# The sums with v inside a chunk: from vector products and reductions to small TensorE products, woven among the large ones

## The chip, the cores and the metric

The kernel runs on one core of one Trainium2 chip. The metric is the device time of one execution in microseconds (us). Runs are timed several times and the median is given; beside them stands one execution taken with the hardware profiler, whose rows are used below. The engines are TensorE (PE in the profile; PEld is its weight load), VectorE (DVE), ScalarE (ACT), GpSimd (POOL) and the queue SP, which issues all transfers of this kernel.

## What is computed

Eight sequences (batches) of 256 tokens with 512 features pass through a transformer layer (self attention, cross attention with a context, a feed-forward block of 2048) and then through a layer of the RWKV kind. All of it is float32. The change lies in the recurrence of the second layer, which has 32 heads of 16 channels:

```python
def step(s, rkvw):                      # s: one 16 x 16 state per batch and head
    r_t, k_t, v_t, w_t = rkvw           # u, a fixed factor per channel
    a = k_t[..., :, None] * v_t[..., None, :]
    out = jnp.einsum('bhi,bhij->bhj', r_t, u * a + s)
    s = a + w_t[..., :, None] * s
    return (s, out)
_, out = jax.lax.scan(step, s0, rkvw)   # over the 256 tokens
```

Then `out` is normalized per head, multiplied by a gate `g`, projected by `Wo` and added to the input (the time mix); a second normalization, a shift by one token and three 512 x 512 products follow (the channel mix). r, k, v, g come from 512 x 512 products, the decay w from a small two-step product.

## The kernel before

The whole program is unrolled. Every instruction carries a priority; a list scheduler orders each engine's instructions when the program is built: where several are ready by its clock, the lowest priority number goes first. On the chip each engine then follows its list in order, and SP its list of transfers.

First come the 32 jobs of the transformer layer (four phases of eight batches), then the second layer, in stages per batch that are named by a letter. `SEQ` (L71) gives the order in which the stages are written down; `AT` and `PACE` (L85, L86) set their priorities: stage s of batch b stands at `PACE * (b + AT[s])` from a common base. In the time mix (`TimeMix`, L539 to L847):

- **a**: normalization, transposition, the low-rank mixing coefficients (L564, L566, L575).
- **b**: gate g and product k. **e**: product v, decay w (L667, L675), product r. Each 512 x 512 product of 256 tokens is written as three products of rounded parts (`mm3`, L185 to L187): 72 with 512 columns and 48 with 256 columns in one batch. k, v, r and w go to DRAM.
- **c**: the 256 tokens are cut into 16 chunks of 16; a partition holds one chunk of four heads (8 x 16 = 128 partitions). For every chunk, GpSimd multiplies r, k and the decays and VectorE sums over the channels, which gives `A`, the 16 x 16 lower triangle of coefficients between the tokens of the chunk, for four heads (L713 to L749; four levels m = 1, 2, 4, 8). Then, for each token t of a chunk, GpSimd multiplies row t of `A` with the t + 1 values of v so far (L755), and VectorE sums (L762): this is the part of `out` that stems from the own chunk. It goes to DRAM as `on`, with the scaled k (`ks`), the scaled r (`r0`) and the decay of a chunk (`dd`).
- **d**, the stage between chunks: the states of all chunks from small 32 x 32 products of k and v (L807), a scan over the chunks on VectorE (L824), 32 x 32 products of r with the states (L834), added to `on` under a mask for the two chunks that share 32 partitions (L837), then the norm per head (L839 to L847) and the store of `yg`.

The channel mix has stages **f** (gate, product o, normalization, mixing) and **g** (products fr, fk, fv and the result); f waits for `yg` of its batch.

SBUF is dealt out by hand: `SLOTS` names the buffers that a tile of a phase may take, `BANKS` the PSUM banks. A tile that is given a taken buffer waits until the last reader of the old tile is done. Stage d has one PSUM bank `wtp` and two banks `up`; `A` has one buffer; the tiles `in` (k, r, w and v of stage c) have four.

An fp32 matmul (L807, L834, L564, L566, L667, L675, L780) stands in the profile as two matmul records, a product of rounded parts as one.

## Time and profile before

| | us |
|---|---|
| median of 3 runs (lowest, highest) | 1974.78 (1973.81, 1986.49) |
| profiled execution, its own time | 1982.31 |
| its span, first to last instruction | 1980.5 |
| second layer: stage b of batch 0 begins (first L652) | 1193.7 |
| last product of stage e, batch 7, copied out (last L643) | 1641.2 |
| stage c: first L713, last L762 | 1239.2, 1794.4 |
| last L834 of stage d, batch 7 | 1819.1 |

From 1193 us to the end the engines are busy: PE 655, DVE 581, POOL 527, ACT 366 of 787.5 us. Busy time of PE is a union of records that overlap, so it is no measure of how much the array does; at half the clock the same product is busy for almost twice as long. The granted clock (1.0 or 0.5 in stretches of 3.41 us, or multiples) is read from the clock column of a table by stages, and from the distance of the starts of two equal products in the timeline. Idle time of an engine costs nothing where another one is the bottleneck.

| first start per batch, us | 0 | 1 | 2 | 3 | 4 | 5 | 6 | 7 |
|---|---|---|---|---|---|---|---|---|
| b (L652) | 1194 | 1242 | 1289 | 1343 | 1405 | 1470 | 1528 | 1593 |
| c (L713) | 1239 | 1311 | 1383 | 1454 | 1521 | 1589 | 1662 | 1728 |
| d (L807) | 1323 | 1395 | 1462 | 1529 | 1599 | 1670 | 1736 | 1779 |
| g (L924) | 1690 | 1742 | 1791 | 1830 | 1863 | 1896 | 1929 | 1962 |

### The profile page before, as it was taken

To read this page: it belongs to the slowest core of one execution; us is meant where nothing else is said; L and a number is where in the kernel's file an instruction comes from. 1 tells how busy PE (TensorE), PEld (TensorE's weight loads), DVE (VectorE), ACT (ScalarE), POOL (GpSimd) and SP (SyncE) were. 2 spreads that over 40 slices of the span, in tenths; PEclk is the share of its full clock that TensorE was granted. 3 is DMA by queue.
4 is the path that set the end of the run, shared out by engine and by line. 5 is a ranking of instruction groups with operands and counts; after the bars stand their busy time and mean duration, and the time that the engine had idled before them with its cause. 6 is when DMAs were issued, how large, how long until landed. Compare 5 with 4: busy or idle time off the path is not lost.

```text
span 1980.5 us, 38765 instructions
## 1 busy us (share of the span) xinstructions
PE 1756.4 (89%) x14576; PEld 1471.8 (74%) x14576; DVE 1379.7 (70%) x3211; ACT 1106.5 (56%) x2745; POOL 747.5 (38%) x550
## 2 busy tenths in 40 slices
PE   4999999989999998999999988888889895789877
PEld 4777777777777776799999976676777673677766
DVE  4777777776778687665654454669678788888554
ACT  3877777887778688532332334354464454355342
POOL 2111111121221221232311100898899999992000
PEclk9999999999999999999999998988898886888888
DMA  6644444656555556322311133454556476442210
GB/s 189 158 125 119 118 118 125 190 142 164 132 146 143 133 135 207 110 90 69 107 65 64 54 128 103 116 142 125 157 138 165 130 195 184 142 108 97 75 64 22
DMA packets 237170, 247.35 MB, mean 125 GB/s; under 512 B 156292, under 2 KB 159244, under 8 KB 236983
## 3 DMA queue, kind: packets, MB, share of 16 engines
q1 hardware_dynamic: 236982, 244.87, 44.7%
q8 instruction: 115, 1.88, 0.4%
q14 instruction: 73, 0.59, 0.1%
HBM read 118.71 MB, written 58.98 MB: 90 GB/s over the span
## 4 chain that ended last, share of the span: by engine, by line
PE 60%; DVE 15%; DMA 6%; ACT 6%; POOL 5%; issue 3%; SPq 3%; POOLq 0%; DVEq 0%; ACTq 0%
PE o L185 8%; PE o L186 8%; PE o L187 8%; PE mm L185 5%; PE mm L186 4%; PE mm L187 4%; PE tr L366 3%; PE out L187 3%; PE out L186 3%; PE out L185 3%; DVE e L359 3%; POOL X L755 2%; PE cx L375 2%; DVE e L357 2%; PE sc L355 2%
## 5 line engine op out<-in xcount | busy, mean ns | idle before, releaser
L362 ACT ACTIVATE e<-e,mx 128x256 f32<-128x256 f32 x512 | 256.7, 506 | 43.0 <-DVE mx L359 42.0
L357 DVE TENSOR_TENSOR e<-sc,mc 128x512 f32<-128x512 f32 x256 | 172.1, 683 | 111.8 <-PE sc L355 56.2
L227 POOL TENSOR_TENSOR u<-y,u 128x1024 fp32r<-128x1024 f32 x32 | 78.5, 2452 | 440.8 <-ACT u L226 440.6
L359 DVE CUSTOM_DVE_ANT_0 e<-e,mn 128x256 f32<-128x256 f32 x512 | 220.6, 473 | 1.0
L755 POOL TENSOR_TENSOR X<-A,in 128x128 f32<-128x128 f32 (+14 forms) x120 | 209.3, 1779 | 14.7 <-DVE ob L762 12.4
L185 PE MATMUL o<-whi,s 128*128 128x512 f32 x320 | 148.4, 464 | 49.4 <-ACT s L890 31.8
L366 PE MATMUL tr<-ident,e 128*128 128x128 f32 x1024 | 174.7, 285 | 18.0 <-ACT e L362 14.7
L185 PE MATMUL mm<-u,whi 128*128 128x256 f32 x512 | 153.7, 301 | 14.3 <-DVE s L319 7.8
L370 ACT COPY pt<-tr 128x512 f32<-128x512 f32 x256 | 147.0, 582 | 34.6 <-PE tr L366 33.9
L366 PEld LDWEIGHTS tr<-ident,e 128*128 128x128 f32 x1024 | 122.3, 144 | 49.2 <-ACT e L362 24.2
L186 PE MATMUL mm<-u,whi 128*128 128x256 f32 x512 | 147.5, 288 | 4.0 <-POOL u L227 4.0
L185 PE MATMUL o<-u,whi 128*128 128x256 f32 x512 | 144.7, 287 | 3.1 <-ACT whi L171 1.6
L187 PE MATMUL mm<-u,wlo 128*128 128x256 f32 x512 | 147.0, 287 | 0.0
L186 PE MATMUL o<-u,whi 128*128 128x256 f32 x512 | 144.0, 283 | 0.0
L187 PE MATMUL o<-u,wlo 128*128 128x256 f32 x512 | 144.0, 283 | 0.0
L186 PE MATMUL o<-wlo,s 128*128 128x512 f32 x320 | 141.4, 442 | 0.0
L293 POOL TENSOR_TENSOR xr<-xr,row 128x512 f32<-128x512 f32 x48 | 65.7, 1388 | 186.0 <-DMA xr<-in_x 81.1
L355 PE MATMUL sc<-stk 128*128 128x256 f32 x512 | 118.0, 322 | 19.3 <-DVE e L357 13.9
L187 PE MATMUL o<-whi,s 128*128 128x512 f32 x320 | 134.4, 438 | 0.6 <-DVE s L891 0.5
L507 ACT ACTIVATE hf<-o,cv 128x256 f32<-128x256 f32 x128 | 59.8, 475 | 117.8 <-PE o L187 115.0
L197 POOL TENSOR_SCALAR rstd<-mv 128x2 f32<-128x2 f32 x48 | 17.2, 357 | 281.2 <-DVE mv L195 260.5
L185 PEld LDWEIGHTS o<-whi,s 128*128 128x128 f32 x320 | 70.0, 219 | 68.8 <-ACT s L890 33.3
(324 smaller groups left out, 5296.3 us busy)
## 6 DMA issues: line engine op xcount, KB each, us to landing
stk<-s SPq DMA_DIRECT2D x512, 128.0 KB, 2.4
x<-x SPq DMA_DIRECT2D x40, 512.0 KB, 4.7
x<-xr SPq DMA_DIRECT2D x24, 512.0 KB, 3.6
xr<-x SPq DMA_DIRECT2D x16, 512.0 KB, 4.8
w<-in_w SPq DMA_DIRECT2D x16, 512.0 KB, 6.7
w<-v SPq DMA_DIRECT2D x32, 256.0 KB, 3.2
x<-in_x SPq DMA_DIRECT2D x8, 512.0 KB
xr<-in_x SPq DMA_DIRECT2D x8, 512.0 KB, 3.6
```

The source lines that it names most:

```text
L185: TE.matmul(o, ah, bh, start=first, stop=False)
L186: TE.matmul(o, ah, bl, start=False, stop=False)
L187: TE.matmul(o, al, bh, start=False, stop=last)
L227: (eng or V).tensor_tensor(lo, y, r32(hi), ALU.subtract)
L293: G.tensor_tensor(x[:, t, :], x[:, t, :], r, ALU.add)
L355: TE.matmul(sc[:, t, :], qs[hm][:, hc, t * P : (t + 1) * P], ks[hm][:, hc, :], start=True, stop=True)
L357: V.tensor_tensor(e, sc, mc, ALU.mult)
L359: V.tensor_tensor_reduce(e[:, t, :], e[:, t, :], mn[:, t, :], 1.0, 3.0e38, ALU.add, ALU.min, accum_out=mx[:, kk2, hc, t : t + 1])
L362: S.activation(pr[:, t, :], e[:, t, :], AF.Exp, bias=mx[:, kk2, hc, t : t + 1], scale=-1.0, accum_out=sums[:, kk2, hc, t : t + 1])
L366: TE.transpose(pt_ps[:, kk, t * P : (t + 1) * P], pr[:, t, kk * P : (kk + 1) * P], ident)
L370: S.copy(pt, pt_ps)
L755: G.tensor_tensor(Y.rearrange("p (h j s) -> p h j s", h=4, j=16), A[:, t, 0:n, :].rearrange("p s h -> p h s").unsqueeze(2).broadcast_to([P ...
```

## The change

In stage c the products and sums with v (L755, L762), the transposed copy of v (L703) with its transfers, and the store of `on` are gone. `A` is now one tile for all batches, zeroed once, so that its upper triangle stays zero; it is laid out by column and goes to DRAM. The tile `in` has three buffers instead of four. In stage d the part of `out` from the own chunk is a product: for each half t of the tokens (128 rows), each of 32 heads and each group pr of 32 partitions (two chunks), a 32 x 32 block of `Ax` (the two triangles of a pair of chunks, spread by ScalarE with a mask so that the other quadrants are zero) by 32 x 16 values of v, into one bank: 2 x 32 x 4 = 256 fp32 matmuls per batch. A group pr takes rows and output partitions 32 pr to 32 pr + 31.

Stage d becomes a generator. `weave` only puts it on a list; `between(n)`, called in the k loops of the large products of all phases, counts their columns and emits the next piece of the generator when as many columns have gone by as the last `yield` asked for. The pieces take the priority of the stage that they are woven into. The yields of one batch add up to about 54,000 columns, the products of stages b and e of a batch have about 53,000. Stage f of batch b first emits what is left of d up to b (`finish`). `SEQ`, `AT` and `PACE` are set anew: with 4000 numbers between batches, the priorities follow the order in which the stages are written.

```diff
-        "in:a16-a19 ob:a12 vm:a20,a21 r0t:a22 sts:a23 on_:a2 "
+        "in:a16-a18 At:a19 Ax:a12 vm:a20,a21 r0t:a22 sts:a23 on_:a2 "
...
-    "a0 b0 a1 e0 c0 b1 a2 e1 c1 d0 b2 a3 e2 c2 d1 b3 a4 e3 c3 d2 b4 a5 e4 c4 d3 b5 a6 e5 c5 d4 b6 a7 e6 c6 d5 b7 "
-    "e7 c7 f0 d6 f1 g0 d7 f2 g1 f3 g2 f4 g3 f5 g4 f6 g5 f7 g6 g7"
+    "a0 b0 a1 e0 c0 b1 a2 e1 c1 b2 a3 d0 e2 c2 b3 a4 d1 e3 c3 b4 a5 d2 e4 c4 b5 a6 d3 e5 c5 b6 a7 d4 e6 c6 b7 d5 e7 c7 "
+    "f0 d6 f1 g0 f2 d7 g1 f3 g2 f4 g3 f5 g4 f6 g5 f7 g6 g7"
...
-AT = {"a": -0.5, "b": -8.75, "e": 1.8, "c": -9.5, "d": -9.3, "f": 6.25, "g": 7.75}
-PACE = 1000
+AT = {"a": -0.75, "b": 0, "e": 0.5, "c": 1, "d": 0, "f": 8.6, "g": 9.7}
+PACE = 4000
...
+    woven, columns = [], [0]
+    def between(n):
+        columns[0] += n
+        while woven and columns[0] >= woven[0][1]:
+            columns[0] -= woven[0][1]
+            was, phase[0] = phase[0], "time"
+            woven[0][1] = next(woven[0][2], None)
+            if woven[0][1] is None:
+                woven.pop(0)
+            phase[0] = was
+    def weave(b, steps):
+        if not woven:
+            columns[0] = 0
+        woven.append([b, 0, steps])
+    def finish(b):
+        while woven and woven[0][0] <= b:
+            columns[0] = woven[0][1]
+            between(0)
...
                     mm3(o[:, oo, :], wh[:, k, cs], wl[:, k, cs], xh[:, k, :], xl[:, k, :], k == 0, k == KC - 1)
+                    between(3 * T)
...
                     mm3(o, xh[:, k, ts], xl[:, k, ts], wh[:, k, :], wl[:, k, :], u == 0 and k == 0, u == n - 1 and k == KC - 1)
+                    between(3 * D)
...
                 TE.matmul(tp_[0:64, 0, :], d1[:, k, :], y[:, k, :], start=k == 0, stop=k == KC - 1)
+                between(4 * T)
...
-            vt = wt("in", [P, 64, 16])
-            for h in range(2):
-                vh = staged([P, 8, 64])
-                nc.sync.dma_start(out=vh, in_=vd.rearrange("e (c t) d -> (e c) t d", t=16)[:, 8 * h : 8 * h + 8, :])
-                S.copy(vt[:, :, 8 * h : 8 * h + 8].rearrange("p d s -> p s d"), vh)
-
-
-            A = wt("A", [P, 16, 16, 4])
+            if b == 0:
+                self.A = wt("A", [P, 16, 4, 16])
+                G.memset(self.A, 0.0)
+            A = self.A
...
-                return bass.AP(A.tensor, A.offset + 64 * t + 4 * s_, [A.ap[0], *dims])
+                return bass.AP(A.tensor, A.offset + 64 * s_ + t, [A.ap[0], *dims])
...
-            V.tensor_reduce(part(0, 0, [[68, 16], [1, 4]]), X.rearrange("p (t g i) -> p t g i", t=16, i=16), AX.X, ALU.add)
+            V.tensor_reduce(part(0, 0, [[65, 16], [16, 4]]), X.rearrange("p (t g i) -> p t g i", t=16, i=16), AX.X, ALU.add)
...
-            ob = wt("ob", [P, 16, 64])
-            for t in range(16):
-                n = t + 1
-                Y = wt("X", [P, 1024])[:, : 64 * n] if t else ob[:, 0, :]
-                G.tensor_tensor(
-                    Y.rearrange("p (h j s) -> p h j s", h=4, j=16),
-                    A[:, t, 0:n, :].rearrange("p s h -> p h s").unsqueeze(2).broadcast_to([P, 4, 16, n]),
-                    vt[:, :, 0:n].rearrange("p (h j) s -> p h j s", j=16),
-                    ALU.mult,
-                )
-                if t:
-                    V.tensor_reduce(ob[:, t, :], Y.rearrange("p (d s) -> p d s", s=n), AX.X, ALU.add)
+            ad = dtile(f"ad_{b}", [P, 16, 64])
+            nc.sync.dma_start(out=ad, in_=A.rearrange("p s h t -> p s (h t)"))
...
-            return back(kb, "ks"), back(rb, "r0"), dd, vd, back(ob, "on")
+            return back(kb, "ks"), back(rb, "r0"), dd, vd, ad
 
         def d(self, b, got):
-
-            ksd, r0d, dd, vd, ond = got
+            weave(b, self.steps(b, got))
+        def steps(self, b, got):
+            ksd, r0d, dd, vd, ad = got
             dn = staged([16, D])
             nc.sync.dma_start(out=dn.rearrange("c (e d) -> c e d", e=8), in_=dd.rearrange("e c d -> c e d"))
+            s0t = wt("s0t", [P, KC, 16])
+            nc.sync.dma_start(out=s0t, in_=a["ctx"][b, 2:18, :].rearrange("r (a j) -> (r a) j", j=16).rearrange("(g p) j -> p g j", p=P))
+            ks = [self.n_tile(ksd, t, "ks") for t in range(2)]
+            At = wt("At", [P, 2, 8, 64])
+            for t in range(2):
+                nc.sync.dma_start(out=At[:, t], in_=ad.rearrange("(e u c) s x -> u (c s) e x", e=8, u=2)[t])
+            r0 = [self.n_tile(r0d, t) for t in range(2)]
+            o = wt("on_", [P, 2, D])
+            yield 8 * T
...
+            r0t = wt("r0t", [P, KC, T])
+            yield 4 * T
+            for k2 in range(2):
+                tp = bank("wtp", [P, 2, T])
+                for kk in range(2):
+                    for t in range(2):
+                        TE.transpose(tp[:, kk, t * P : (t + 1) * P], r0[t][:, (2 * k2 + kk) * P : (2 * k2 + kk + 1) * P], ident)
+                S.copy(r0t[:, 2 * k2 : 2 * k2 + 2, :], tp)
+                if not k2:
+                    yield 8 * T
+            vms, vns = [], []
+            for t in range(2):
+                vms.append(wt("vm", [P, 2, D]))
+                vns.append(self.n_tile(vd, t))
+                for par in range(2):
+                    S.activation(vms[t][:, par, :], vns[t], AF.Copy, scale=pm[:, 2 + par : 3 + par])
+            def spread(t):
+                Ax = wt("Ax", [P, 32, 2, 16])
+                for par in range(2):
+                    S.activation(Ax[:, :, par, :], At[:, t].rearrange("p e (h t) -> p (e h) t", t=16), AF.Copy, scale=pm[:, 2 + par : 3 + par])
+                return Ax
+            yield 28 * T
...
-            r0 = [self.n_tile(r0d, t) for t in range(2)]
-            r0t = wt("r0t", [P, KC, T])
-            to_t(r0, lambda k2, tp: S.copy(r0t[:, 2 * k2 : 2 * k2 + 2, :], tp), "wtp")
-            o = wt("on_", [P, 2, D])
-            for t in range(2):
-                nc.sync.dma_start(out=o[:, t, :].rearrange("p (e d) -> p e d", e=8), in_=ond[:, t * P : (t + 1) * P, :].rearrange("e p d -> p e d"))
+                if r_ == 3:
+                    Ax = spread(0)
+                yield 9 * T
...
-            for q in range(4):
+            def inside(t):
+                av = bank("wtp", [P, D])
+                for h in range(32):
+                    js = slice(16 * h, 16 * h + 16)
+                    for pr in range(4):
+                        rws = slice(32 * pr, 32 * pr + 32)
+                        TE.matmul(av[rws, js], Ax[rws, h].rearrange("p c t -> p (c t)"), vns[t][rws, js], start=True, stop=True)
+                    if h % 4 == 3:
+                        if h == 31:
+                            S.copy(o[:, t, :], av)
+                        yield 5 * T
+            def across(q):
...
+                    if t and q:
+                        chosen(q, op)
+                    elif t:
+                        first.append(op)
+                    yield 6 * T
+            def chosen(q, op):
                 ov = o.rearrange("p t (g q j) -> p (t g) q j", q=4, j=32)[:, :, q]
                 for par in range(2):
                     V.scalar_tensor_tensor(ov, op.rearrange("p t g c j -> p (t g) c j")[:, :, par], pm[:, 2 + par : 3 + par], ov, ALU.mult, ALU.add)
+            first = []
+            yield from inside(0)
+            Ax = spread(1)
+            yield from across(0)
+            yield from inside(1)
+            chosen(0, first[0])
+            for q in range(1, 4):
+                yield from across(q)
...
+                if stage == "f":
+                    finish(b)
...
+    finish(len(jobs))
```

## The prediction

> **What bounds the kernel now.** I read the page's busy times first, then a table by stages, then who PE waits for, then the timeline. The change touches only the second layer, so I cut that at the start of b for batch 3 (1342.5 us), at the end of e for batch 7 (1641) and at the end of d for batch 7 (1830):
>
> ```profile
> core 0: us, PE busy (x) PEld busy (x) DVE busy (x) ACT busy (x) POOL busy (x), PEclk, DMA share, GB/s
> 1193.00:1342.50 149.50, 129.47 (x899) 105.73 (x901) 93.41 (x145) 70.71 (x155) 98.90 (x74) 0.90 0.46 121
> 1342.50:1641.00 298.50, 260.70 (x3275) 210.34 (x3268) 244.94 (x412) 143.86 (x317) 276.57 (x192) 0.86 0.58 158
> 1641.00:1830.00 189.00, 143.98 (x2038) 117.40 (x2037) 159.82 (x285) 93.78 (x202) 147.41 (x96) 0.81 0.44 128
> 1830.00:1980.50 150.50, 120.93 (x615) 99.83 (x613) 82.63 (x151) 57.67 (x112) 3.72 (x8) 0.88 0.16 53
> ```
>
> GpSimd is full from 1342 to 1795 us (277 of 298.5, then 147 of 153) and starts a stage c every 69 to 73 us. But stage c is not what b and e wait for: their starts lie only 48, 47 and 53 us apart at first and 58 to 65 us later, so they run ahead of c (c of batch 0 starts 45 us after b, of batch 7 135 us after). There PE is the nearest bound, busy for 261 of 298.5 us at a mean clock of 0.86. What it waited for in that stretch:
>
> ```profile
> PE up L834 <- DVE sts L824: 7.7, 6, 3.2
> PE o L185 <- ACT s L632: 7.5, 7, 2.9
> PE lo L575 <- ACT xa L576: 4.2, 3, 2.9
> PE o L675 <- POOL n L670: 3.1, 1, 3.1
> ```
>
> No single wait rules (37.8 us idle in all). The chain that ended last says the same: from 1193 us on, the three product lines hold 35% of it, L755 only 6.0%, 47 us. So taking 26 us of GpSimd out of each batch is no gain of 26 us.
>
> **The clock.** After the 128-record block of L834 the large products start 0.43 us apart instead of 0.235:
>
> ```profile
> 1495.32 0.40 PE L185 MATMUL o<-whi,s 128*128 128x512 f32 x1
> 1495.56 0.39 PE L186 MATMUL o<-wlo,s 128*128 128x512 f32 x1
> ...
> 1496.35 3.42 PE L834 MATMUL up<-sts,r0t 32*32 32x64 f32 x128
> ...
> 1500.80 0.63 PE L185 MATMUL o<-whi,s 128*128 128x512 f32 x1
> 1501.23 0.63 PE L186 MATMUL o<-wlo,s 128*128 128x512 f32 x1
> ```
>
> The table over 1495.9 to 1499.3 gives clock 1.00, over 1499.3 to 1502.7 it gives 0.50: a stretch filled with 32 x 32 products is followed by half clock, though PE was busy in it. The Trainium skill, "TensorE: Matmul & The Clock Gate", Part 1, ties the half rate to a window in which PE is idle; here the row decides against that reading, and by the page alone the weaving would win nothing on this term.
>
> **What the change costs on PE, per batch.** 256 fp32 matmuls are 512 records. No row shows a 32 x 32 by 16. The nearest is L807, 32 x 32 by 64, in a block between products:
>
> ```profile
> 1528.66 0.28 PE L186 MATMUL o<-s,whi 128*128 128x256 f32 x1
> 1528.78 0.28 PE L187 MATMUL o<-s,wlo 128*128 128x256 f32 x1
> 1528.99 0.99 PE L807 MATMUL up<-vm,ks 32*32 32x64 f32 x64
> 1529.91 0.39 PE L185 MATMUL o<-s,whi 128*128 128x256 f32 x1
> 1530.13 0.29 PE L186 MATMUL o<-s,whi 128*128 128x256 f32 x1
> ```
>
> 64 records take 0.92 us, 14.4 ns each. Within a group of four they start 7 ns apart, and the group repeats after 56 ns, the time in which 64 columns stream. With 16 columns the cost lies between 7 and 14.4 ns, if the four row groups run beside each other as the four column groups of L807 do; L834, with strided operands, has 27 ns (3.42/128), the far end. I take 10 ns: **+5.1** us (3.6 to 13.8).
>
> Each small block also pays for the switch: from 1528.78 to 1530.13 are 1.35 us, less 0.92 and two products of 0.12 leave 0.19. Stage d had about 10 blocks per batch (L780, L217, L807 and L834 bunched); now 3 + 4 + 16 + 8 = 31. 21 x 0.19 = **+4.0** us (0, where the scheduler bunches them, to 6).
>
> The Trainium skill, "TensorEngine Tiling (Array Packing)", Instruction Overhead, speaks against the change: some 60 cycles per matmul, however few columns. By that, 512 x 25 ns would be an estimated 12.8 us per batch instead of 5.1; the 7 ns between starts above contradict it for tiles that run together.
>
> **Work taken off or hidden.** GpSimd loses L755, 211.9 us in all, 26.5 per batch; VectorE L762, 89.2 us, 11.1 per batch. Neither is on PE's list, both shorten queues that feed it. ScalarE loses two L703 (1.10 us each) and gains four spreads like L795 (0.72) and two copies (0.6): +1.9 us per batch, at 144 of 298.5 us hidden; without cover it would be 15 us. Transfers: the two loads of v (256 KB each) go; `A` out and in takes the place of `on` out and in, same sizes, same 3 to 4 us. On SP nothing new stands ahead of other loads. The one memset of `A` is one GpSimd instruction, under the 2.5 us of an L713. VectorE's sums into the new layout I hold at L743's 1.21 us: 64 outputs of 1024 inputs. With three `in` buffers nothing is lost, v's was the fourth. Stage c shrinks to 38 to 42 us of GpSimd work (L713 to the last L743), plus store and load of 4 us each: about 50, below the 60 of b and e, so c never holds d.
>
> **The sum**, against the span of 1980.5:
>
> *To 1342.5:* no d but the first; 0.
>
> *1342.5 to 1641*, 4.5 stages d: cost 4.5 x 9.1 = +41. The waits of L834 for the scan and of L807 for L795 go, since the pieces after the scan come one by one and inside(0) covers it: 7.7 + 1.5 = -9. Half-clock stretches after L834 blocks come to about 31 us, of which some 25 hold large products; at full clock that is -12. The rest of PE's waits, 28 us, with about 37 us of half clock behind them, hang on VectorE, ScalarE and GpSimd queues (VectorE is busy for 245 of 298.5 us) in which stage c went first and now comes after a and e; I count half, -14 -9 = -23, somewhat less as small pieces slow the return to full clock: -20. Together **0**.
>
> *1641 to 1830:* 3.2 stages d, +29, and 45 us in which PE is idle. 24.5 of these lie in the 50 us before the first g, while the weights of the channel mix land; the rest of d of batch 5 and that of 6 can fill it. From the end of o (L902) to the mixing (L911) f takes 19.0, 16.4, 15.8 and 9.6 us for batches 0 to 3 and 8.4 after GpSimd has fallen idle (its normalization steps L197, L198 queue behind pieces of 2.5 us): 27 us late, on the path where no g runs beside. PE's work at full clock is about 120 us here (3.3 x 24 for f and g, 3.2 x 12.4 for d), then 149; at 90% it fits 166: **-23**.
>
> *From 1830:* f and g 33 us apart by their own chain, GpSimd busy 3.7 us: 0.
>
> Span 1957.5. The profiled execution (1982.3) lies 7.5 above the median, so the forecast is 1974.8 - 23 = **1952 us**.
>
> **Rivals.**
>
> *The pieces fill nothing* (no change, 1965 to 1990). Two gains above, -20 and -23, are judged, not measured. If f's chain and the weights still set the stretch after 1641, its 29 us of added work eat the gain: 1975. For it speaks that the last stretch, with GpSimd idle, still needs 33 us for 24 us of products.
>
> *GpSimd was the bound after all* (1900 to 1935). If the 47 us of L755 on the chain and some of L762 come out whole, and the added PE work falls into the 82 us that PE idles from 1342.5 to 1830, the time is 1974.8 - 60 = 1915. Against it: PE takes most of the chain.
>
> *Small products clog PE* (slower, 1995 to 2040). The four row groups of the new product may not run together: no row of before has a block with changing row groups. At L834's 27 ns the cost is 13.8 instead of 5.1 per batch; eight batches add 70 us, of which the idle before the first g hides 20 to 25. It decides from about 17 ns on. The clock pushes the same way: once at half, it came back after a stretch with 2.9 us or more of large products in 3.4 us, or 2.5 with 0.9 small, but not with 2.7 and 0.7 (1622 to 1626). Woven pieces (0.9 us per 0.7 us of product for L834) can hold it there. Price: 1952 + 70 = 2022.
>
> That the weaving does not do what it says, because the scheduler bunches ready pieces, costs up to the 12 us of clock and saves switches: inside the forecast.
>
> **How the numbers follow.** Runs of this kernel tell about 1% from no change (20 us). Forecast 0.30, GpSimd bound 0.13, no change 0.22, clogged PE 0.35: faster 0.43, same 0.22, slower 0.35. The far end of the per-record cost and both rivals set the range, 1903 to 2028; the likeliest case alone has 1936 to 1955.
>
> **What would show it.** The new matmul at 7 to 14 ns per record, blocks of about 0.3 us; L834 in blocks of 32 records and no half clock behind them; GpSimd below 65% from 1342 on; e of batch 7 ending near 1641; first g less than 49 us later, the next ones near 42 apart. Wrong if the new records stand above 17 ns, if the mean clock falls below 0.86, or if VectorE waits for GpSimd took the place of what went.

## The result, and the profile after

| | before | after |
|---|---|---|
| median, us (lowest to highest) | 1976.74 (1973.81 to 1986.49) | 2052.28 (2046.90 to 2053.08) |
| profiled execution, its span | 1982.31, 1980.5 | 2046.90, 2045.1 |
| ratio | | **1.037** (95%: 1.034 to 1.040) |

The kernel became 3.7% slower, outside the range of the forecast. (Before has four timed executions here, one more than above.) Line numbers from here on are those of the changed kernel: the products are L209 to L211 (185 to 187 before), the products of k and v L849 (807), the new ones L872, those of r with the states L887 (834), the scan L863 (824). The page of after, its first, second and third part:

```profile
span 2045.1 us, 46720 instructions
...
PE 1854.6 (91%) x18672; PEld 1525.6 (75%) x18672; DVE 1301.5 (64%) x3091; ACT 1122.9 (55%) x2777; POOL 536.3 (26%) x423
...
q8 instruction: 147, 2.41, 0.5%
```

and the same lines of before:

```profile
span 1980.5 us, 38765 instructions
...
PE 1756.4 (89%) x14576; PEld 1471.8 (74%) x14576; DVE 1379.7 (70%) x3211; ACT 1106.5 (56%) x2745; POOL 747.5 (38%) x550
...
q8 instruction: 115, 1.88, 0.4%
```

What was to be taken off is off: GpSimd loses 211 us, VectorE 78. PE has 4096 records more and is busy for 98 us more. The queue that brings instructions carried 32 packets more for 7955 instructions more, some 250 in a packet; that will matter below.

The table by stages of after, cut at the start of b for batches 3 and 7 and where d of batch 7 is past its last L887, and at last the whole second layer (columns as in the prediction's table):

```profile
1193.00:1345.50 152.50, 135.31 (x1271) 107.45 (x1269) 88.20 (x132) 70.90 (x155) 80.11 (x62) 0.91 0.50 132
1345.50:1647.90 302.40, 275.75 (x4903) 214.56 (x4900) 175.38 (x301) 134.63 (x303) 157.74 (x117) 0.83 0.48 126
1647.90:1892.00 244.10, 216.77 (x4095) 161.84 (x4094) 153.66 (x285) 120.00 (x248) 72.41 (x55) 0.81 0.37 110
1892.00:2045.00 153.00, 126.48 (x648) 104.03 (x646) 83.47 (x154) 56.45 (x109) 3.72 (x8) 0.91 0.17 57
...
1193.00:2045.10 852.10, 754.31 (x10909) 587.88 (x10907) 500.72 (x870) 381.99 (x815) 313.99 (x241) 0.85 0.40 110
```

Before, with the same cuts (the outer two stretches stand in the prediction):

```profile
1342.50:1592.60 250.10, 217.29 (x2632) 177.27 (x2625) 203.48 (x350) 116.43 (x261) 232.32 (x161) 0.87 0.53 145
1592.60:1830.00 237.40, 187.38 (x2682) 150.47 (x2681) 201.28 (x346) 121.21 (x258) 191.65 (x127) 0.81 0.51 147
...
1193.00:1980.50 787.50, 655.08 (x6815) 533.30 (x6813) 580.80 (x990) 366.03 (x783) 526.59 (x369) 0.86 0.44 124
```

52 of the 65 us are lost between b of batch 3 and b of batch 7: 250.1 us became 302.4, 13 per batch. PE's busy time there grew by 58 us while the clock *fell*, from 0.87 to 0.83. GpSimd is down to 52% there, and PE waits for none of its results (the list of waits below names it nowhere): relief came, and no time with it. In the stretch after, idle time of PE (length less busy) went from 50 to 27 us, as hoped, and the stretch is longer all the same, at a clock of 0.81 as before.

**An account in three terms.** PE's time from 1193 us on can be cut into *idle* (length less busy), *half* (half of the busy time that lies in stretches of half clock, which is what the clock costs) and *work* (the rest: the busy time as it would be at full clock). I took busy and half clock from each record's start and end and from the steps of the granted clock. The three add up to the stretch, so differences between kernels can be read off term by term. It is a reckoning on one profiled execution each, and it takes a factor of two for the half clock, where the starts of two 512-column products stand 0.235 us apart at full clock and 0.43 at half, and small records are slowed less still; so some of what is work stands under *half*. Executions of one kernel also differ in the clock. As a check on all of them, the span times one less the mean granted clock is what the clock took away over the whole kernel: a median of 140 us in before (130 to 151 in the 16 executions beside e1 to e4), 161 in after (153 to 164).

| | stretch | work | half | idle |
|---|---|---|---|---|
| before | 787.5 | 569.8 | 85.3 | 132.4 |
| after | 852.1 | 647.6 | 106.7 | 97.8 |
| difference | **+65** | **+78** | **+21** | **-35** |
| the forecast's terms, summed in this way | -23 | +69 | -41 | -51 |

(Forecast: work 41, and 149 less the account's 121 in the stretch after 1641, +28. Half: -12, then -6 out of the -20, and -23 after 1641, where all 22.6 us of half clock went with "PE's work at full clock". Idle: -9, -14, and 45 less the 17 that 90% leave, -28.) The price on PE was nearly right. What was to be won in return was not: the clock term has the wrong sign and holds 62 of the 88 us of error. By stretch: from b of batch 3 to b of batch 7 work, half and idle changed by +42, +16 and -6 us, and from there to the end of d by +20, +10 and -23. Half clock rose in both stretches in which it was to fall.

Who PE waited for from 1345.5 to 1647.9, in after (in total us, times, longest):

```profile
PE wtp L872 <- DMA w<-v: 6.2, 2, 3.3
PE wtp L872 <- issue: 6.1, 3, 2.7
PE o L209 <- ACT s L658: 5.1, 4, 1.7
PE up L887 <- issue: 4.3, 3, 1.9
PE wtp L872 <- ACT Ax L838: 1.9, 1, 1.9
PE up L887 <- DVE sts L863: 1.7, 2, 1.4
```

The wait for the scan did fall, from 7.7 to 1.7 us, as forecast. In its place stand waits for nothing that the profile shows ("issue"), 22.2 us from 1193 us on against 0.3 before, and one for the transfer of v.

### The profile page after: what moved, and what is told of

The parts are those of the page before. It is cut to its first block, busy times and chain, and to the rows that moved or that the text cites. A ratio compares the mean times of both kernels' runs of the same rounds, so it can differ in the third digit from the quotient of the medians.

```text
span 2045.1 us, 46720 instructions
## 1 busy us (share of the span) xinstructions
PE 1854.6 (91%) x18672; PEld 1525.6 (75%) x18672; DVE 1301.5 (64%) x3091; ACT 1122.9 (55%) x2777; POOL 536.3 (26%) x423
## 4 chain that ended last, share of the span: by engine, by line
PE 67%; DVE 12%; ACT 7%; DMA 4%; issue 4%; POOL 3%; SPq 2%; POOLq 0%; DVEq 0%; ACTq 0%
PE o L209 9%; PE o L211 8%; PE o L210 8%; PE mm L209 4%; PE mm L210 4%; PE mm L211 4%; PE tr L392 3%; PE out L211 3%; PE out L209 3%; PE out L210 3%; DVE e L385 3%; PE up L887 2%; PE cx L401 2%; DVE e L383 2%; PE sc L381 2%
## 5 line engine op out<-in xcount | busy, mean ns | idle before, releaser
L392 PE MATMUL tr<-ident,e 128*128 128x128 f32 x1024 | 173.6, 284 | 18.3 <-ACT e L388 14.6
L209 PE MATMUL o<-whi,s 128*128 128x512 f32 x320 | 155.3, 485 | 31.2 <-ACT s L959 21.4
L209 PE MATMUL mm<-u,whi 128*128 128x256 f32 x512 | 154.5, 302 | 11.8 <-DVE s L345 5.6
L211 PE MATMUL mm<-u,wlo 128*128 128x256 f32 x512 | 147.8, 289 | 0.0
L209 PE MATMUL o<-u,whi 128*128 128x256 f32 x512 | 143.9, 285 | 2.8 <-ACT hf L533 1.9
L211 PE MATMUL o<-u,wlo 128*128 128x256 f32 x512 | 143.5, 282 | 0.8 <-DVE wlo L196 0.8
L211 PE MATMUL o<-whi,s 128*128 128x512 f32 x320 | 139.9, 451 | 2.4 <-DVE s L659 2.3
L533 ACT ACTIVATE hf<-o,cv 128x256 f32<-128x256 f32 x128 | 59.9, 475 | 119.6 <-PE o L211 116.9
L221 POOL TENSOR_SCALAR rstd<-mv 128x2 f32<-128x2 f32 x48 | 18.3, 382 | 374.1 <-DVE mv L219 353.6
L381 PEld LDWEIGHTS sc<-stk 128*128 128x128 f32 x512 | 82.6, 199 | 43.8 <-DVE e L383 24.7
L760 POOL TENSOR_TENSOR X<-in 128x1024 f32<-128x1024 f32 x48 | 113.3, 2392 | 3.5 <-DVE A L766 3.4
```

The lines of the kernel that those rows point to most:

```text
L209: TE.matmul(o, ah, bh, start=first, stop=False)
L211: TE.matmul(o, al, bh, start=False, stop=last)
L381: TE.matmul(sc[:, t, :], qs[hm][:, hc, t * P : (t + 1) * P], ks[hm][:, hc, :], start=True, stop=True)
L392: TE.transpose(pt_ps[:, kk, t * P : (t + 1) * P], pr[:, t, kk * P : (kk + 1) * P], ident)
L760: G.tensor_tensor(X.rearrange("p (i s d) -> p i s d", i=ni, s=m), rb[:, t0 : t0 + ni, :].unsqueeze(2).broadcast_to([P, ni, m, 64]), kb[:, ...
```

## The experiments

Each was timed beside the kernel before on the same chip; ratios are to it, and it stood at 1980 to 1982 us there, some 5 us above its 1976.74 beside after, so across rows the ratios are the better measure. e4, e5 and e9 leave out three quarters of the sum within a chunk and serve as measures of time alone. The accounts of the runs, from 1193 us on (of *idle*, "issue" is what the waits put down to it):

| run | median us | ratio (95%) | work | half | idle | issue |
|---|---|---|---|---|---|---|
| before | 1976.74 | | 569.8 | 85.3 | 132.4 | 0.3 |
| after | 2052.28 | 1.037 (1.034, 1.040) | 647.6 | 106.7 | 97.8 | 22.2 |
| e1, not woven | 2108.83 | 1.065 (1.062, 1.067) | 582.0 | 134.3 | 203.3 | 59.9 |
| e2, not woven, old order | 2108.77 | 1.064 (1.062, 1.067) | 582.4 | 132.9 | 201.3 | 62.8 |
| e3, weaving alone | 1991.07 | 1.004 (1.002, 1.005) | 575.4 | 98.9 | 130.2 | 5.6 |
| e4, quarter of the records | 1991.57 | 1.004 (1.001, 1.006) | 623.6 | 81.9 | 93.9 | 0.5 |
| e5, quarter, not woven | 1979.19 | 0.999 (0.998, 1.001) | 584.0 | 85.1 | 115.9 | 14.6 |
| e6, coarse pieces | 2054.56 | 1.036 (1.032, 1.039) | 646.7 | 103.8 | 110.4 | 18.3 |
| e7, fine pieces | 2016.36 | 1.017 (1.014, 1.021) | 651.2 | 76.0 | 94.4 | 22.5 |
| e8, products in two batches | 2006.95 | 1.012 (1.009, 1.015) | 579.1 | 102.7 | 132.2 | 16.5 |
| e9, wide, not woven | 2116.81 | 1.069 (1.066, 1.071) | 617.3 | 112.8 | 189.2 | 38.5 |
| e10, very fine pieces | 2037.97 | 1.028 (1.025, 1.031) | 651.2 | 81.3 | 102.8 | 22.3 |
| e11, 64 x 64, fine | 2076.02 | 1.047 (1.045, 1.050) | 664.6 | 119.6 | 92.7 | 1.2 |
| e12, 64 x 64, not woven | 2098.53 | 1.058 (1.056, 1.060) | 605.0 | 144.1 | 155.7 | 1.2 |
| e13, half the spacing | 2070.22 | 1.045 (1.041, 1.048) | 624.3 | 151.5 | 99.7 | 3.6 |
| e14, fine, half the spacing | 2079.60 | 1.048 (1.043, 1.052) | 623.0 | 165.5 | 101.2 | 12.8 |
| e15, fine, 5/4 of the spacing | 2010.99 | 1.015 (1.010, 1.020) | 648.1 | 87.1 | 80.4 | 21.0 |

### Taking the change apart

**e1**, the products without the weaving:

```diff
-            weave(b, self.steps(b, got))
+            for _ in self.steps(b, got):
+                pass
```

> The changed kernel with its new order and priorities, but stage d emitted in one piece where it stands in the order, not woven. Theory A (price of records and switches): PE is full, and the time added is that of the new matmul records (about 6 us per batch) and of some 22 more blocks per batch at 0.19 us each. Then without the weaving the switches go: 2052 - 8 x 4 = about 2020. Theory B (the clock): small pieces between the large products keep PE at half clock (34% of the time from 1345 to 1648 us, 26% before); without the weaving that goes as well: about 1995 to 2005. Theory C (the order): the new priorities cost the time, not the pieces: 2040 to 2060.

**e2** is e1 with `SEQ`, `AT` and `PACE` as before.

> The sums with v as small TensorE products for all batches, stage d in one piece, and SEQ, AT and PACE of the kernel before. Theory A: 1976 + 8 x 6 = about 2025, less what the relief of GpSimd gives back after 1641 us (up to 25): 2000 to 2025. Theory B: the same, 2000 to 2025, with the mean clock in the stretch of b and e as before (0.86 to 0.87). Theory C (order): 1955 to 1980, since GpSimd and VectorE are relieved and the order is the old one.

**e3**, the weaving and the new order without the products: the sums with v stay on GpSimd and VectorE (the removed lines of stage c put back, `inside` and `spread` taken out, 40 T of waiting columns in place of each `inside`).

> Weaving and new order as in the changed kernel, but the sums with v stay on GpSimd and VectorE as before (the pieces of the new products leave only their columns). Theory A: 2052 less 8 x 6 for the records and 16 switches x 8 x 0.19 = 24: about 1980. Theory B: the other pieces still hold the clock down, about 2000 to 2020. Theory C: 2030 to 2060, and GpSimd is the bound again besides.

e1 and e2 agree within 0.1 us: without the weaving the new order plays no part. e3 is 0.4% slower than before. It shows what became of the gain that the forecast had credited to the weaving: nothing came. Idle time is the same within 2 us. Half clock is up by 13.6 us in the account, but the profiled execution of e3 is the slowest of its seven; over all seven the clock took away a median of 143 us, against 140 in before. By the ratios the new products cost some 128 us unwoven (6.5%) and some 66 woven (3.7% less 0.4%); so the weaving does help, by some 54 us, but only against a price that it did not bring down to what the work is. Of the price unwoven, the account of e1 puts 12 us under work, 49 under half clock and 71 under idle time.

### What the unwoven products cost

The timeline of e1, PE alone (start, us, group; in brackets idle time before it):

```profile
1445.39 2.10 PE L850 MATMUL up<-vm,ks 32*32 32x64 f32 x126 [1.22 <-issue]
...
1449.30 1.90 PE L873 MATMUL wtp<-w,Ax 32*32 32x16 f32 x128 [1.78 <-issue]
1452.77 1.09 PE L873 MATMUL wtp<-w,Ax 32*32 32x16 f32 x66 [1.57 <-issue]
...
1460.60 1.90 PE L873 MATMUL wtp<-w,Ax 32*32 32x16 f32 x128 [1.90 <-issue]
1464.35 0.34 PE L873 MATMUL wtp<-w,Ax 32*32 32x16 f32 x9 [1.84 <-issue]
```

128 records run for 1.9 us (at half clock here), and then PE stands for 1.6 to 1.9 us with nothing to wait for. 128 records with their weight loads are 256 instructions; a packet of the instruction queue has 16384 bytes, by the page's counts some 250 instructions. In this stretch such packets start at 1442.95, 1447.10, 1450.38, 1453.85, 1457.98 and 1461.75 us, 3.3 to 4.2 us apart. So in a long run of small products PE gets 128 records in some 3.6 us, 28 ns each; the reading is that instructions are the limit, however short the records are. The 128 records of L834 before, at 27 ns, nearly hid this, and the 14.4 ns in a block of 64 records could not show it. The Trainium skill, "Runtime: NRT & Kernel Launch", Instruction fetch mechanics, tells of blocks of 256 instructions whose loading is hidden by the pace of issue; the block size agrees, the hiding does not.

Three runs test it.

**e5**: e1 with 64 columns in one record for four heads and so 128 records per batch instead of 512 (the other three blocks of `Ax` are left out).

```diff
-                    js = slice(16 * h, 16 * h + 16)
-                    for pr in range(4):
+                    js = slice(16 * h, 16 * h + 64)
+                    for pr in range(0 if h % 4 else 4):
```

> The unwoven kernel (e1, 2109 us) with a quarter of the new matmuls, 64 columns each instead of 16 (three quarters of this sum are not the right ones). In e1 the block of new matmuls runs 128 records at 12 ns and then PE waits 1.6 to 1.9 us for nothing that the profile shows, again and again; 128 records with their weight loads are 256 instructions, one 16 KB transfer of the instruction queue. Theory S (instruction supply): a long run of small products goes at the pace of these transfers, about 3.6 us for 128 records, however long each takes; 3 transfers fewer per batch: 2109 - 8 x 3 x 3.6 = about 2023. Theory A (array time): 512 x 12 ns less 128 x 14 ns = 4.3 us per batch: about 2074.

**e9**: e1 with all 512 records, each of 64 columns (four heads then write the same columns, so three quarters of the sum are left out).

> The unwoven kernel e1 with all 512 new records per batch, but each with 64 columns of v instead of 16 (so this sum is not the right one): the same instructions, four times the columns. Theory S (instruction supply): nothing changes, 2109 within 8 us, runs of 128 records still 3.5 to 3.7 us apart, with a shorter wait between them (0.07 us longer records: 1.9 us of run become about 2.0). Theory A (array time): 512 x 8 x 3 ns more or above: 2120 to 2150.

**e12**: 64 x 64 blocks (four chunks under four masks) instead of 32 x 32, 256 records per batch, not woven; **e11** the same, woven in 32 pieces of 8 records.

> The same 64 x 64 products in the unwoven kernel e1: 256 records per batch instead of 512, the full result. Theory S: two transfers of instructions fewer per batch; by their pace alone 2109 - 58 = 2051, by the step from e1 to e5 (130 us for 384 records a batch) 2022. Theory A: 512 x 12 ns less 256 x 14 ns: 2109 - 20 = 2089.

> Woven as in e7, but the new products take 64 rows and 64 columns of the array (four chunks, triangles spread by four masks): 128 matmuls, 256 records per batch instead of 512, 32 pieces of 8 records; the full result. ScalarE has 16 spreads of about 0.48 us per batch instead of 4 of 0.72: +4.8 us, hidden. Theory S: half the instructions, so about half of what is left over the weaving alone (2016 against 1991): 1995 to 2005. Theory A: array time per record stays or rises, 2005 to 2020.

e5: with a quarter of the records all of the loss is gone (ratio 0.999), waits for issue fell from 59.9 to 14.6 us, the clock's loss from 134 to 85. e9: with the same number of records, four times the columns cost only 8 us more, and the waits before L873 fell from 43.6 to 20.4 us: time on the array took the place of waiting, as the supply theory says. The pace shows it best: at full clock, a run of 128 of its records that starts at 1609.13 us takes 1.99 us and the next run starts 3.47 us after it; in e1, at half clock and with a quarter of the columns, that is 3.47 too (1449.30 to 1452.77). Not all of the small difference in time is the supply, though: in the account e9 has 35 us more work, 14 less idle time and 22 less half clock, and the theory had said nothing of the clock. e12 did not do what it was made for. Half as many instructions leave no wait for issue, but the record itself became three times as long, and twice that at half clock:

```profile
1447.79 3.91 PE L877 MATMUL wtp<-w,Ax 64*64 64x16 f32 x128
...
1453.54 7.01 PE L877 MATMUL wtp<-w,Ax 64*64 64x16 f32 x128
```

30 ns and 55 ns a record. So e12 does not speak against the supply; it swapped it for a cost as high, and e11, woven, shows the same.

### Woven: fewer records, other pieces

**e4** is the edit of e5 in the woven kernel, with the same part of the sum left out.

> The changed kernel with a quarter of the new matmuls (of every four heads only the first block of Ax is used, with 64 columns of v instead of 16, so three quarters of this sum are not the right ones; the number and place of the pieces stay). 128 records of 64 columns, about 14 ns each, instead of 512 of about 11: 1.8 instead of 6 us per batch. Theories A and B: 2052 - 8 x 4.2 = about 2018 (if PE is full), with B a little less as shorter blocks hold the clock less: 2005. Theory C: 2040 to 2055, since PE is not what is waited for.

The 66 us of the woven products are back for 3072 records fewer (ratio 1.004, as e3). The account splits the 53 us between the two profiled spans: work 24, half clock 25, idle 4. As work, a woven record less saves 24/3072 = 7.8 ns net, since the records that are left are longer; the clock takes as much again. Behind b of batch 7, 359 us are left, where before has 388, e3 (woven, GpSimd not relieved) 397 and after 397: the relief of GpSimd at the end can be worth some 29 us, and the full products eat it.

**e6** and **e7** change the size of a piece, not the mean spacing: 4 pieces of 128 records or 32 of 16, instead of 16 of 32; **e10** has 64 of 8. The edit of e7 (e6 has every 16th head and `20 * T`, e10 every head and `5 * T // 4`):

```diff
-                    if h % 4 == 3:
+                    if h % 2 == 1:
...
-                        yield 5 * T
+                        yield 5 * T // 2
```

> The changed kernel with the new products in 4 pieces per batch of 128 records, each asked for after four times as many columns, instead of 16 pieces of 32 records. Theory W (switches): 12 blocks fewer per batch at 0.19 us: 2052 - 18 = 2034. Theory S (supply): a piece is then one whole transfer of instructions in a run, and PE waits up to 1.8 us after it: 2052 - 18 + up to 58 = 2055 to 2090.

> The changed kernel with the new products in 32 pieces per batch of 16 records instead of 16 of 32, after half as many columns each. Theory W: 16 blocks more per batch at 0.19 us: 2052 + 24 = 2076. Theory S: the supply keeps up better, of the 22 us that PE waits without a shown reason before the small products some go: 2052 - 22 + 24 = 2054 or less.

> The changed kernel with the new products in 64 pieces per batch of 8 records, one per head, after a quarter of the columns each. Theory S: as from 2052 to 2016 with half-size pieces, the small products are spread still more evenly over the large ones, so less waiting and less half clock: 1990 to 2010. Theory W (switches): 32 more blocks per batch than e7 at 0.19 us: 2016 + 48 = 2064.

Coarse pieces are like after; fine ones win some 36 us, against the theory that each small block costs its switch; very fine ones give half of it back. The account is plain for e7: work +4, idle -3, half clock **-31** us. The waits for issue are the same 22 us. What the pieces change is the clock, and all executions say so: it took away a median of 161 us in after, 155 in e6 and 122 in e7. (e10's profiled execution is the fastest of its four and has the highest clock of them, so its account shows too little of its loss against e7. Over all four the clock took 138 us, 16 more than in e7, of 22 us by the medians of the times. Work is the same in both accounts, so it isn't switches; why the clock is lower is open.)

**e8**, the new products only in batches 6 and 7, where GpSimd is late (the tiles of both ways share two buffers in it, `At` with the copy of v and `Ax` with `ob`): 16 us slower than e3.

> Woven as in the changed kernel, but only batches 6 and 7 take the new products; batches 0 to 5 keep the sums on GpSimd and VectorE. If the cost is that of the new products in the stretch of b and e, where PE is full, and the relief of GpSimd pays only after the last e, as I forecast for the stretch from 1641 us: the 1991 of the weaving alone less 15 to 29: 1962 to 1976, at or a little below the kernel before. If the new products cost their 7.6 us per batch everywhere: 1991 + 15 = 2006.

Waits for issue rose by 11 us and work and half clock by 4 each; no gain in idle time shows. Placing the products at the end alone does not turn them into a gain.

### Spacing: does a piece hold the half clock?

**e13** halves every number of columns that stage d yields, **e14** does so with the fine pieces, **e15** has fine pieces and 5/4 of the spacing.

```diff
-                        yield 5 * T
+                        yield 5 * T * 1 // 2
```

> The whole result; every number of columns that stage d gives back is halved, so a piece comes after half as much product work and the pieces of a batch lie in half as many products, with twice their share there. In the trace of the change, stretches of 3.41 us (the step in which the granted clock changes) that began at full clock and held 0.5 to 2.2 us of 32 x 32 products never dropped (0 of 60), those at half clock with as much stayed at half (19 of 23), and those at half clock with under 0.5 us returned (21 of 22). Theory H (the pieces do not bring the half clock, they hold it once it is there): fewer stretches have pieces, so fewer are held; the loss by half clock from 1193 us on, 107 us in the change and 85 before, falls to some 90: 2035. Theory S (instruction supply, 22 us of waits ascribed to issue in the change): the records come closer together, the waits grow to some 35 us and the clock does not move: 2065.

> The whole result; pieces of 16 records as in the run with fine pieces (2016), the spacing halved: 16 records after each 320 columns, which is the mean share of the change with the pieces halved again in the middle of stage d. Theory H: as with fine pieces, at most 10 us better: 2006 to 2016. Theory S: the records come twice as fast as in the fine run, so the waits for issue grow by some 13 us and the gain of the fine pieces goes: 2030 to 2050.

> The whole result; pieces of 16 records with the spacing widened by a quarter, which is about all the product work that a batch has. Theory H: more stretches hold pieces, each with a smaller share; some 0.8 us of small products per 3.41 us still hold the half clock, so 2016 to 2035. Theory S: the records come more slowly, the waits for issue (22 us in the fine run) fall by 5 to 10 us: 2006 to 2011.

Both theories failed in a number: e13 came out at 2070, near the 2065 of the supply theory, but for the opposite reason. Waits for issue fell to 3.6 us; the loss by half clock rose from 107 to 151 us. With fine pieces the same halving costs 63 us (2016 to 2080), and half clock more than doubles, 76 to 166. Theory H had the mechanism and a wrong inference: I took it that fewer stretches with pieces would be fewer stretches held; instead, denser pieces hold nearly every one. The table by stretches of e13 shows both sides, four stretches at full clock, then four at half; PE is busy throughout in all eight:

```profile
1460.94:1464.35 3.41, 3.41 (x55) 2.28 (x53) 0.00 (x0) 1.42 (x3) 3.33 (x3) 1.00 0.84 194
1464.35:1467.76 3.41, 3.41 (x94) 2.65 (x93) 3.05 (x5) 1.41 (x5) 3.41 (x3) 1.00 0.46 121
1467.76:1471.17 3.41, 3.41 (x82) 2.82 (x82) 2.51 (x6) 2.87 (x10) 3.41 (x4) 1.00 0.02 5
1471.17:1474.59 3.42, 3.42 (x69) 2.30 (x70) 0.66 (x2) 2.25 (x6) 3.42 (x5) 1.00 0.00 0
...
1423.39:1426.80 3.41, 3.41 (x74) 1.97 (x73) 0.00 (x0) 0.00 (x0) 0.00 (x0) 0.50 0.00 0
1426.80:1430.22 3.42, 3.42 (x100) 2.50 (x99) 0.97 (x2) 2.40 (x4) 0.00 (x0) 0.50 0.57 119
1430.22:1433.63 3.41, 3.41 (x77) 2.45 (x80) 0.97 (x2) 0.00 (x0) 0.00 (x0) 0.50 0.65 193
1433.63:1437.04 3.41, 3.41 (x87) 2.46 (x83) 0.97 (x2) 0.00 (x0) 0.00 (x0) 0.50 0.02 5
```

The first four hold 1.0 to 1.6 us of 32 x 32 products each and stay at full clock; the last four hold 1.0 to 1.9 us and stay at half. The first four are of L849 and the last of L872 and L887, so the kind of product might be what decides. It is not: over the seven woven traces with all of the 32 x 32 products in every batch (after, e6, e7, e10, e13 to e15), stretches with 0.5 to 2.2 us of small products, over four fifths of it L872, dropped from full clock in 0 of 95 cases, and with 0.5 us or more stayed at half in 58 of 66; for L849 it is 8 of 149 and 26 of 28, for L887 4 of 117 and 75 of 85. Such a mixture keeps whatever clock it finds. Counted over each trace, from 1193 us to the end of d (a stretch is 3.41 us; "small" is the time in it that L849, L872 and L887 take, L807 and L834 in before, without what overlaps the record ahead; the rows on small products are for stretches with PE idle for at most 0.5 us; a cell says how many were followed by half clock; of those at full clock with under 0.5 us of both, none was):

| clock now, what the stretch holds | before | after | e7 | e13 | e14 | e15 |
|---|---|---|---|---|---|---|
| full, PE idle for over 0.5 us | 24 of 41 | 19 of 30 | 15 of 29 | 12 of 25 | 10 of 23 | 17 of 32 |
| full, small 0.5 to 2.2 us | 0 of 26 | 0 of 60 | 2 of 70 | 4 of 45 | 1 of 40 | 2 of 69 |
| full, small over 2.2 us | 4 of 9 | 6 of 7 | 3 of 5 | 1 of 3 | 3 of 3 | 4 of 4 |
| half, PE idle for over 0.5 us | 19 of 19 | 17 of 17 | 16 of 16 | 15 of 15 | 20 of 20 | 10 of 10 |
| half, small under 0.5 us | 3 of 28 | 1 of 22 | 1 of 17 | 4 of 20 | 5 of 17 | 2 of 19 |
| half, small 0.5 us or more | 4 of 7 | 22 of 26 | 9 of 13 | 54 of 55 | 61 of 63 | 19 of 25 |

Woven pieces hardly ever bring the half clock: it comes after idle time, and after long blocks of small products. They hold it: 4 such stretches before, 22 after, 54 in e13. 18 more stretches of 3.41 us at half rate are worth some 31 us. e15 makes the count from the other side: with wider spacing b and e keep the pace of before (b of batch 7 at 1600 us, 1593 before, 1648 in after), but d of batch 7 ends at 1917 us instead of 1882, and the end is late by that. There is no more product work in a batch into which it could be spread further.

No version beat the kernel before; the best that do all of the new products in every batch are e15 and, within the noise, e7, 1.5% and 1.7% slower. No run took away the idle time that the half clock follows; whether that would turn the change into a gain was not tried.

## Why the prediction was wrong

**The step that failed** is the clock, at two places of the sum: "Half-clock stretches ... at full clock that is -12", and, after 1641, "PE's work at full clock is about 120 us here, ... then 149; at 90% it fits 166". The second takes for granted a full clock in a stretch whose row shows 0.81. Idle time after b of batch 7 fell by 23 us, close to the 28 that this step needs, and PE did become busy for about 90% (216.8 of 244.1 us); but the clock stayed at 0.81, and the loss by it rose by 10 us there instead of going. The first place has the rule, which I read off the trace before, on the wrong side: a block of L834 is followed by half clock, so pieces in place of the block would spare it. They do not bring it, but it still comes after idle time, and then they keep it: 22 of 26 such stretches in after, 4 of 7 before. The term was also too large for its own trace. Of the 24 stretches of half clock from 1342 to 1641 us in before (82 us), only four (14 us) follow a stretch filled with 32 x 32 products in which PE stood for less than 0.5 us. The forecast's 31 us come out only with five more (17 us, from 1618.8 us on), and those follow a stretch in which PE stood for 1.95 us. e3 shows the outcome for the weaving alone: the clock took away 143 us in it and 140 in before, no gain.

**The price per record** held: 126 records in one block of after,

```profile
1504.06 0.74 PE L647 MATMUL tp<-xa,m2h 128*128 128x256 f32 x4
1504.72 1.41 PE L872 MATMUL wtp<-w,Ax 32*32 32x16 f32 x126
1505.95 0.29 PE L887 MATMUL up<-sts,r0t 32*32 32x64 f32 x2
```

take 1.23 us from start to next start, 9.8 ns each, where 10 were taken; over all 4096 I count 11 ns at full clock and 17 to 18 at half. The four row groups do run beside each other. What no row of before could show is that this pace holds for 128 records only.

**The switches** held as a sum by two errors: I put the blocks at 10 per batch before and 31 after, by the trace those of the 32 x 32 products were 5 and 25 per batch (43 and 198 in all). 155 more at 0.19 us are 29 us; the forecast's 4.0 in each of 7.7 stages are 31. The 0.19 us itself, read from one block, is right for the new product: 13 blocks of 32 records between large products at full clock in after put these 0.46 us further apart, 0.26 from the first start to the last and 0.20 for the switch. e4 against e3 agrees roughly: 96 blocks more (18 us) and 1024 records of 64 columns (22 us), beside 48 us more of work.

**Waits.** The scan's went nearly as forecast (7.7 to 1.7 us in the stretch, of the -9). Of the "other waits", -20, nothing is left in the sum: between b of batches 3 and 7 idle time fell by 6 us (32.8 to 26.7), and issue waits of 10.4 us are new there. Without the 22 us of issue over the whole layer idle time would have fallen by 57, near the 51 forecast; that they only replaced other waits is possible and was not tried.

**Hidden work** was hidden: among what PE waited for from b of batch 3 to b of batch 7, ScalarE's new work and the transfers of `A` show up nowhere but in 1.9 us of L872 for `Ax`.

**The signs listed.** New records at 7 to 14 ns: yes. L834 in blocks of 32 without half clock behind them: no, pieces bunch (126 records above, then 40 of L887). GpSimd below 65%: yes, 52%. e of batch 7 ending near 1641: no, its decay product starts at 1684 us instead of 1613; first g 62 us later (1690 to 1752) where less than 49 was said, and the next 55 and 63 us apart, not 42. The clock falls below 0.86 in the two stretches where stage d is woven, 0.83 and 0.81.

**The rivals.** "Small products clog PE", with 35 in 100, was the right one in direction, and 2022 in size lies between forecast and result. Its first reason, row groups that do not run together, is refuted; its second, that woven pieces can hold the half clock, is what the runs show. The prediction gave that reason no price of its own. "GpSimd was the bound after all" falls: 211 us less on GpSimd, and none of the four stretches of after became shorter; only the end of e4 did. (Stage c started every 66 to 73 us before, not every 69 to 73; nothing hangs on it.)

## What to carry to other kernels

When small products are put between large ones, look at the granted clock first: a mixture that holds full clock also holds half clock. So the places to work on are the idle time that half clock follows (no run here tried that) and stretches of about 3.4 us nearly free of small products, after which full clock returned in 21 of 22 cases in after. Don't cost stretches of PE at full clock unless their row says so. A pace that is read from a block of 64 records is not the pace of 500: in runs of 128 records (256 instructions) and more the supply of instructions set it here, at 28 ns per record, so the number of records counts (e5), and fewer records only help if each does not grow with it (e12).

## What had not been expected of the hardware

- The clock has a memory. In e13 stretches with 0.5 to 2.2 us of small products and no idle time kept the full clock in 41 of 45 cases, and those with 0.5 us or more that began at half clock stayed there in 54 of 55. The Trainium skill, "TensorE: Matmul & The Clock Gate", Part 1, has the full rate return after about one busy window; these 54 stretches were busy throughout or nearly so and it did not, so the measurement decides against the page where 32 x 32 products lie in the window.
- In runs of small products PE stands for 1.6 to 1.9 us after each 256 instructions (e1), 3.6 us per packet of 16384 bytes.
- A 64 x 64 record of 16 columns takes 30 ns at full clock where a 32 x 32 one takes 9.8, for the same 16 columns.
- Weaving in pieces of 16 records instead of 32, at the same mean spacing, gave some 36 us. Between the two profiled executions, 30.5 us apart, half clock makes up all of it (31); that half clock was held in 9 stretches with small products instead of 22 is counted, why it was is open.
